# Key gathers of an AUGRU spread over its half steps, whole rows for the first steps, score rows on another queue, weights sorted after a branch

## The chip, the cores and the metric

The kernel runs on one core of one Trainium2 chip. The metric is device time of one execution in microseconds (us), lower is better. The engines named below are PE (matmul), DVE (vector), ACT (scalar, activations), POOL (GpSimd) and SP (mostly issues DMA transfers). A group of DMA transfers is issued on the queue of the engine that names it; gathers by a list of row numbers (indirect DMAs) are issued by POOL, one for 128 rows.

## The reference

1024 sequences of 100 items, 128 features each. Cut to what matters:

```python
# GRU over t: keys[:, t] = h after step t
def gru_step(h, x_t): ...                 # 3 gates, 128 -> 128, on x_t and h
keys = scan(gru_step, h0, items)
feat = concat([keys, q, keys - q, q * keys])      # q: the item embedding
score = mlp(feat, att_W0..W2, relu); score = where(mask, score, -inf)
attn = softmax(score, axis=time)
pooled = einsum('bt,btd->bd', attn, keys)
att_seq = pooled.T[:T]                    # feature t of a sequence weights step t
def augru_step(h, (x_t, a_t)):
    r = sigmoid([h, x_t] @ Wr.T + br); u = sigmoid([h, x_t] @ Wu.T + bu)
    h_hat = tanh([h * r, x_t] @ Wh.T + bh)
    u = a_t * u
    return (1 - u) * h + u * h_hat
aug = scan(augru_step, h0, keys with att_seq)
attention_feature = aug[at the sequence's length - 1]
out = mlp([user, item, hist_sum, item * hist_sum, attention_feature], ph_W0..W2, sigmoid)
```

## The kernel before, in words

Everything is kept transposed: features on 128 partitions, sequences along the free axis, in two halves of `HB` = 512 sequences that are worked in turn. One step of one half is called a half step.

**First phase, GRU** (to about 1580 us). The outer loop runs over t, the inner over the two halves. A half step has ten matmuls of 128x128 by 512 in f32 for the gates (L438) and a few for the attention score (L506, L507, L678). `transpose` turns the new state by 32x32 blocks on DVE into `kt` (L482), and every four steps one DMA on SP's queue stores the tile (128 partitions, 16 blocks of 32 sequences, 4 steps of 32 features each) to a table `keys_d` in DRAM (L485). `transpose` is followed two steps later by `score`, which spreads one row of `mv` into `s_b` by a DMA on SP's queue (L519); ACT's next write of `mv` (L510) waits for that DMA, and DVE's softmax in blocks reads `s_b`. On SP's queue stand also the loads of inputs `x` (L409) and masks `m` (L414). POOL accumulates `hist` and `pooled` (L425, L426, L598, L599).

**Between the phases.** `weights` forms `att` and stores it to `pooled_d` (L614), in pieces of 32 floats (128 B), on the queues of SP and ACT in turn. `features` and `sort_weights` follow: POOL gathers the rows of `pooled_d` in order of length (L114), PE turns them (L656), DVE copies the result (L658), SP stores it to `att_d`, a matmul with one row of the unit matrix spreads the weights of t = 0 (L661), and ACT copies them to `h3` (L668). Then each engine loads a number that says which of three lists of widths fits the lengths, and branches (L882, L883).

**Second phase, AUGRU** (`augru_phase`, from about 1622 us). Sequences are sorted by length, so a step works on the first w columns of a half only; w falls from 512 by about 5 a step from t = 3 on (482 at t = 8, 276 at t = 48, 30 at t = 96). A half step is six matmuls (L784 and L786: gates r, u and h, each on the key and on the state), three activations on ACT (L793, L796, L800) and five operations on DVE, of which L794 feeds the last matmul. The key of step t comes from the table in groups of steps, `READ` = 4, then 8 each, starting at `FIRST` = 0, 4, 12, 20 and so on. For each block of 32 columns of each half one gather brings 128 rows of 1 KB (32 features by 8 steps) into `rows` (L130). `load_group` issues all gathers of the next group one after the other when the loop reaches a group's first step; the 32 gathers of group 0 run early, during the GRU. `load_key`, two steps ahead, takes a step's key out of `rows` by 32x32 transposes on DVE (L772). `load_att` loads the weight row of a step (L762, SP's queue). When no sequence of a block of 128 is left, `predict` computes its outputs.

The work is written in this order in the program; a tile scheduler places waits and moves independent instructions, and buffer counts (`k3` 6, `u3` 3, `rows` 4) bound how far an engine runs ahead.

Of the kernel before, what the change touches and what calls it, by code (L numbers as in the profile page):

```python
# [19 lines left out]
P = 128  # L20
# [25 lines left out]

G = 4
READ = [G] + [2 * G] * ((T - G) // (2 * G))
FIRST = [sum(READ[:q]) for q in range(len(READ))]

# [12 lines left out]
def kernel(ctx: ExitStack, tc: tile.TileContext, a: dict, out: bass.AP):  # L63
# [18 lines left out]

    nc = tc.nc
# [3 lines left out]
    keys_d = [dram.tile([NK * P, n * R], F32, name=f"keys_d{q}") for q, n in enumerate(READ)]  # L87
# [35 lines left out]
    def load_rows(q, i, width, tiles):  # L123

        n = READ[q]
        r = rows[q, i] = tiles.tile(
            [P, KH, n * R], F32, tag="once" if q == 0 else "rows", name="rows"
        )
        for k in range(-(-width // R)):
            nc.gpsimd.indirect_dma_start(  # L130
# [11 lines left out]
    def gru_phase(pools):  # L142
# [62 lines left out]
        def load_later():  # L205
# [183 lines left out]
        class Half:  # L389
# [85 lines left out]
            def transpose(self, t):  # L475
# [36 lines left out]
            def score(self, t):  # L512
# [6 lines left out]
                nc.sync.dma_start(  # L519
# [83 lines left out]
            def weights(self):  # L603
# [9 lines left out]
                for p in range(P // R):  # L613
                    (nc.scalar if p % 2 else nc.sync).dma_start(  # L614
                        out=to[p], in_=att[p * R : (p + 1) * R]
                    )
# [31 lines left out]

        def sort_weights(i):


            r = xp.tile([P, GH, P], F32, tag="x", name="att_r")
            p = ps.tile([P, HB], F32, tag="g", name="pw")
            for g in range(GH):
                gather(r[:, g, :], pooled_d, g, i)
                nc.tensor.transpose(p[:, ts(g, P)], r[:, g, :], ident)  # L656
            att = hp.tile([P, HB], F32, tag="h", name="att_t")
            nc.vector.tensor_copy(att, p)  # L658
            nc.sync.dma_start(out=att_d[i], in_=att[:T, :])
            first = ps.tile([P, HB], F32, tag="g", name="first")  # L660
            nc.tensor.matmul(  # L661
                first,
                lhsT=ident[:, 0:1].to_broadcast([P, P]),
                rhs=att,
# [291 lines left out]
```

## Time and profile before

| | |
|---|---|
| median of 3 runs | 2459.59 us (2458.4 to 2460.04) |
| the profiled execution | 2471.84 us, its span 2470.0 us |
| mean PE clock granted in it | 0.932 |
| PE busy | 2211.2 us (90%) |
| DVE, POOL, ACT busy | 1723.1, 1276.1, 995.7 us |
| gathers of keys on POOL (L130) | 250, 961 ns each |

The profile comes from one execution. A row of the timeline gives the start and the length of an instruction in us, the engine, the line of the kernel (L130), the operation, what it writes and reads (`out<-in`), the shape and, in brackets, how long its engine had been idle and what it had been waiting for ("issue" is time in which it waited for nothing that the profile shows, "remote" a wait whose releaser is not known). Rows of the 40 slices give busy tenths of each fortieth of the span, about 62 us; PEclk is the clock that PE was granted, in tenths. A row of windows gives start and end, length, busy us and count of each engine, then PE's clock, the DMA engines' busy share and GB/s. A wait row gives the total in us, how often, and the longest.

### The profile page before, as it was taken

The page shows a single profiled execution, that of the slowest core. Times are in us where ns is not written, and L with a number is a line of the kernel's source. Part 1 is how long each engine was busy: PE and PEld are TensorE (multiplying, and loading weights), DVE is VectorE, ACT ScalarE, POOL GpSimd, SP SyncE. Part 2 cuts the span into 40 slices and gives each one's busy share as a digit, 9 for nine tenths or more (in the row PEclk, how much of TensorE's full clock was granted, in tenths as well). Part 3 has the DMA queues.
Part 4 walks back from the last instruction along what each step waited for, and adds up shares of the span by engine and source line. Part 5 has one row for each costly group of instructions (what it writes and reads, how often), then busy time and mean ns, then how long its engine had stood idle before and what let it go on. Part 6 is the DMA issues. An engine that isn't in the chain of part 4 may idle for free. (4 is left out here: it accounts for less than half of the span.)

```text
span 2470.0 us, 22200 instructions
## 1 busy us (share of the span) xinstructions
PE 2211.2 (90%) x6184; PEld 1093.0 (44%) x6184; DVE 1723.1 (70%) x3175; ACT 995.7 (40%) x1729; POOL 1276.1 (52%) x1121
## 2 busy tenths in 40 slices
PE   8998899999999999999999998544987898888898
PEld 3333333344444444444444443211433455667787
DVE  7798667777878777777777787722755666666652
ACT  3343344444444444444444444311332333344432
POOL 0169977666666666666666669364213303222200
PEclk9999999999999999999999999866988988999875
DMA  4533333322222323233222321232223212222210
GB/s 103 136 89 103 111 110 101 86 87 89 85 88 89 86 89 96 85 99 88 85 89 88 87 87 56 58 122 80 83 60 87 82 44 78 73 69 73 55 28 5
DMA packets 228009, 204.22 MB, mean 83 GB/s; under 512 B 41166, under 2 KB 190386, under 8 KB 227874
## 3 DMA queue, kind: packets, MB, share of 16 engines
q1 hardware_dynamic: 213122, 170.40, 24.3%
q0 software_dynamic: 12640, 32.04, 4.5%
q8 instruction: 50, 0.82, 0.1%
q14 instruction: 85, 0.70, 0.1%
q10 hardware_dynamic: 2112, 0.26, 0.1%
HBM read 146.60 MB, written 54.40 MB: 81 GB/s over the span
## 5 line engine op out<-in xcount | busy, mean ns | idle before, releaser
L438 PE MATMUL ps<-x,wih 128*128 128x512 f32 x1200 | 597.1, 607 | 20.2 <-ACT r L450 10.4
L438 PE MATMUL ps<-hn,whh 128*128 128x512 f32 x1188 | 576.0, 594 | 0.4 <-DVE hn L473 0.4
L130 POOL DMA_INDIRECT rows<-keys_d,idx_k x250 | 240.3, 961 | 480.6 <-DVE k L772 375.9
L438 PEld LDWEIGHTS ps<-x,wih 128*128 128x128 f32 x1200 | 221.1, 191 | 347.6 <-issue 272.1
L438 PEld LDWEIGHTS ps<-hn,whh 128*128 128x128 f32 x1188 | 226.0, 190 | 285.8 <-issue 275.6
L510 ACT ACTIVATE mv<-f 128x512 f32<-128x512 f32 x200 | 125.9, 630 | 468.9 <-DVE f L509 304.6
L425 POOL TENSOR_TENSOR xm<-x,m 128x512 f32<-128x512 f32 x200 | 249.6, 1264 | 75.7 <-DMA m<-mask_d 66.9
L786 PE MATMUL ph<-r,wh 128*128 128x512 f32 (+55 forms) x396 | 150.3, 465 | 148.5 <-DVE r L794 92.0
L469 ACT ACTIVATE ps<-ps,bih 128x512 f32<-128x512 f32 x200 | 132.2, 661 | 352.2 <-DVE ps L468 351.0
L599 POOL TENSOR_TENSOR pooled<-pooled,kw 128x512 f32<-128x512 f32 x190 | 258.4, 1360 | 6.7
L426 POOL TENSOR_TENSOR hist<-hist,xm 128x512 f32<-128x512 f32 x200 | 258.7, 1308 | 2.4
L458 DVE SCALAR_TENSOR_TENSOR u<-ps,bhh,r 128x512 f32<-128x512 f32 x198 | 145.6, 735 | 141.5 <-ACT r L450 137.8
L506 PE MATMUL pm<-hn,wk 128*128 128x512 f32 x400 | 209.4, 605 | 33.1 <-DVE f L509 14.8
L584 POOL TENSOR_TENSOR pooled<-pooled,e 128x512 f32<-128x512 f32 x25 | 28.9, 1156 | 385.0 <-ACT e L558 385.0
L471 DVE TENSOR_TENSOR d<-hn,ps 128x512 f32<-128x512 f32 x198 | 135.9, 686 | 119.3 <-ACT ps L469 116.3
L598 POOL TENSOR_TENSOR kw<-kt,e 128x512 f32<-128x512 f32 x190 | 210.9, 1128 | 0.5 <-DVE old L565 0.3
L507 PE MATMUL pm<-kq,wkq 128*128 128x512 f32 x400 | 207.0, 599 | 0.0
L504 DVE TENSOR_TENSOR kq<-hn,item 128x512 f32<-128x512 f32 x200 | 191.7, 958 | 1.3
L800 ACT ACTIVATE ph<-ph,bh 128x512 f32<-128x512 f32 (+48 forms) x200 | 91.9, 459 | 204.4 <-PE ph L786 137.4
L793 ACT ACTIVATE pr<-pr,br 128x512 f32<-128x512 f32 (+49 forms) x198 | 90.5, 457 | 181.9 <-PE pr L786 107.0
L786 PEld LDWEIGHTS ph<-r,wh 128*128 128x128 f32 x396 | 74.9, 217 | 194.9 <-DVE r L794 118.2
L796 ACT ACTIVATE pu<-pu,bu 128x512 f32<-128x512 f32 (+48 forms) x200 | 91.6, 458 | 154.6 <-PE pu L786 70.4
(143 smaller groups left out, 3396.7 us busy)
## 6 DMA issues: line engine op xcount, KB each, us to landing
x<-in_hist_x SPq DMA_DIRECT2D x212, 256.0 KB
keys_d<-kt SPq DMA_DIRECT2D x50, 1024.0 KB
m<-mask_d SPq DMA_DIRECT2D x200, 128.0 KB
rows<-keys_d,idx_k POOLq DMA_INDIRECT x250
s_b<-mv SPq DMA_DIRECT2D x200, 8.0 KB
mask_i<-in_mask SPq DMA_DIRECT2D x8, 200.0 KB
at<-att_d SPq DMA_DIRECT2D x4, 256.0 KB
part_d<-part SPq DMA_DIRECT2D x2, 400.0 KB
```

The lines of the kernel that those rows point to most:

```text
L130: nc.gpsimd.indirect_dma_start(out=r[:, k, :], out_offset=None, in_=keys_d[q], in_offset=bass.IndirectOffsetOnAxis(ap=idx_k[:, k, i : i + ...
L425: nc.gpsimd.tensor_mul(d, x, m)
L426: nc.gpsimd.tensor_add(acc, acc, d)
L438: nc.tensor.matmul(p, lhsT=w[:, g, :], rhs=v, start=(j == 0), stop=(j == len(parts) - 1),)
L458: nc.vector.scalar_tensor_tensor(out=u, in0=ph, scalar=bhh[:, 2:3], in1=r, op0=ALU.add, op1=ALU.mult,)
L471: nc.vector.tensor_sub(d, h, pi)
L504: nc.vector.tensor_mul(kq, h, item[:, self.cols])
L506: nc.tensor.matmul(p, lhsT=wk[i], rhs=h, start=True, stop=False)
L507: nc.tensor.matmul(p, lhsT=wkq[i], rhs=kq, start=False, stop=True)
L598: eng.tensor_mul(d, k, w)
L599: eng.tensor_add(acc, acc, d)
L786: nc.tensor.matmul(p, lhsT=m[:, 0, :], rhs=v, start=False, stop=True)
```

## The change

Five parts.

1. `READ` starts 4, 4, 8, ... For groups 0 and 1 (t = 0 to 7, `WHOLE` = 2) the table holds whole rows of 128 features by 4 steps. `transpose` stores them by four DMAs of 32x16x32 in each half step of t = 0 to 7 (64 in all, 512 pieces of 128 B each) where one of the old form stood for each four steps. One gather brings 128 whole rows of 2 KB, four for a half, and `load_key` turns the key on PE (four transposes) and copies it on ACT.
2. The gathers of the later groups are drawn from a generator, `RATE` = 2 in each half step, and what is left of a group when its predecessor's first step comes is issued at once. Ahead of each gather, from step 1 on, POOL copies one column of the latest `u` into the gather's target, so that the gather waits for that half step's DVE instruction. `load_key` runs one step ahead instead of two. In the AUGRU there are 204 gathers of the old form (250 before, 32 of them early), 8 of whole rows there and 8 early.
3. The `s_b` rows are issued on ACT's queue.
4. `sort_weights` moves behind the branch, after the keys and the gate matmuls of t = 0 (`first_step`); the stores to `pooled_d` are all on SP's queue.
5. `rank`'s comparison and sum become one DVE instruction each.

```diff
-READ = [G] + [2 * G] * ((T - G) // (2 * G))
+WHOLE = 2
+READ = [G] * WHOLE + [2 * G] * ((T - WHOLE * G) // (2 * G))
+READ += [T - sum(READ)] * (sum(READ) < T)
 FIRST = [sum(READ[:q]) for q in range(len(READ))]
+RATE = 2
...
-    keys_d = [dram.tile([NK * P, n * R], F32, name=f"keys_d{q}") for q, n in enumerate(READ)]
+    keys_d = [
+        dram.tile([B, n * P] if q < WHOLE else [NK * P, n * R], F32, name=f"keys_d{q}")
+        for q, n in enumerate(READ)
+    ]
...
     def load_rows(q, i, width, tiles):
 
         n = READ[q]
-        r = rows[q, i] = tiles.tile(
-            [P, KH, n * R], F32, tag="once" if q == 0 else "rows", name="rows"
-        )
+        if q < WHOLE:
+            tag = "whole" if q else "once"
+            r = rows[q, i] = tiles.tile([P, GH, n * P], F32, tag=tag, name="rows")
+            for g in range(GH):
+                gather(r[:, g, :], keys_d[q], g, i)
+                yield
+            return
+        r = rows[q, i] = tiles.tile([P, KH, n * R], F32, tag="rows", name="rows")
         for k in range(-(-width // R)):
+            if later.get("pace") is not None:
+
+                nc.gpsimd.tensor_copy(r[:, k, 0:1], later["pace"])
             nc.gpsimd.indirect_dma_start(
...
                 nc.vector.tensor_scalar(
-                    above, order, own[:, g : g + 1], None, ALU.is_gt
-                )
-                nc.vector.tensor_reduce(rank[:, g : g + 1], above, AX.X, ALU.add)
+                    above,
+                    order,
+                    own[:, g : g + 1],
+                    0.0,
+                    ALU.is_gt,
+                    ALU.add,
+                    accum_out=rank[:, g : g + 1],
+                )
...
-                if n == G - 1:
-                    row, part = divmod(q + 1, 2) if q else (0, 0)
+                if q < WHOLE:
+                    to = keys_d[q][self.cols, :].rearrange(
+                        "(k r) (n a c) -> n a r k c", r=R, n=G, c=R
+                    )
+                    for p in range(P // R):
+                        nc.sync.dma_start(
+                            out=to[n, p], in_=kt[p * R : (p + 1) * R, :, n, :]
+                        )
+                elif n == G - 1:
+                    row, part = divmod(q - WHOLE, 2)
                     nc.sync.dma_start(
-                        out=keys_d[row].rearrange("(k p) m -> p k m", p=P)[
+                        out=keys_d[WHOLE + row].rearrange("(k p) m -> p k m", p=P)[
                             :, self.ks, ts(part, G * R)
                         ],
                         in_=kt.rearrange("p k n c -> p k (n c)"),
...
-                nc.sync.dma_start(
+                nc.scalar.dma_start(
                     out=s_b.rearrange("(p r) f -> p r f", r=R)[:, s - b0, :],
...
-                    (nc.scalar if p % 2 else nc.sync).dma_start(
-                        out=to[p], in_=att[p * R : (p + 1) * R]
-                    )
+                    nc.sync.dma_start(out=to[p], in_=att[p * R : (p + 1) * R])
...
-        for i in range(NH):
-            sort_weights(i)
-
     def augru_phase(pools, widths):
...
-        keys, att = {}, {(0, i): h3[i] for i in range(NH)}
+        keys, att = {}, {}
+        later["pace"] = None
+
+        def first_step(i):
+
+            k = keys.pop((0, i))
+            gates = []
+            for n, f in (("u", AF.Sigmoid), ("h", AF.Tanh)):
+                p = ps.tile([P, HB], F32, tag="g", name=f"p{n}")
+                nc.tensor.matmul(p, lhsT=later["w" + n][:, 1, :], rhs=k, start=True, stop=True)
+                nc.scalar.activation(p, p, f, bias=later["b" + n])
+                gates.append(p)
+            return gates
+
+        def sort_weights(i):
+            r = wp.tile([P, GH, P], F32, name="att_r", bufs=2)
...
         def load_key(t, i):
 
             q = max(j for j, first in enumerate(FIRST) if first <= t)
-            w = -(-widths[t] // R)
-            k = wp.tile([P, KH, R], F32, name="k3", bufs=6)
-            nc.vector.transpose(
-                k[:, :w, :], rows[q, i][:, :w, ts(t - FIRST[q], R)]
-            )
-            k = k.rearrange("p k r -> p (k r)")
+            w, n, r = widths[t], t - FIRST[q], rows[q, i]
+            k = wp.tile([P, HB], F32, name="k3", bufs=6)
+            if q < WHOLE:
+                p = ps.tile([P, HB], F32, tag="g", name="pk3")
+                for g in range(-(-w // P)):
+                    nc.tensor.transpose(p[:, ts(g, P)], r[:, g, ts(n, P)], ident)
+                nc.scalar.copy(k[:, :w], p[:, :w])
+            else:
+                w = -(-w // R)
+                nc.vector.transpose(
+                    k.rearrange("p (k r) -> p k r", r=R)[:, :w, :], r[:, :w, ts(n, R)]
+                )
             keys[t, i] = k
...
             nc.vector.tensor_mul(u, pu, at)
+            later["pace"] = u[:, 0:1]
...
-        def load_group(q):
+        def gathers(q):
             for i in range(NH):
-                all_of(load_rows(q, i, widths[FIRST[q]], kp))
-
-        load_group(1)
-        for t in range(2):
-            for i in range(NH):
-                load_key(t, i)
+                yield from load_rows(q, i, widths[FIRST[q]], kp)
+
         for i in range(NH):
+            load_key(0, i)
+        gates = [first_step(i) for i in range(NH)]
+        for i in range(NH):
+            sort_weights(i)
+        all_of(gathers(1))
+        ahead = gathers(2)
+        for i in range(NH):
+            load_key(1, i)
             load_att(1, i)
         for t in range(T):
-            if t in FIRST[1:-1]:
-                load_group(FIRST.index(t) + 1)
+            if t in FIRST[2:-1]:
+                all_of(ahead)
+                ahead = gathers(FIRST.index(t) + 1)
             for i in range(NH):
                 if t + 2 < T:
                     load_att(t + 2, i)
-                step(t, i)
-                if t + 2 < T:
-                    load_key(t + 2, i)
+                if t:
+                    step(t, i)
+                else:
+                    pu, ph = gates[i]
+                    u = wp.tile([P, HB], F32, name="u3")
+                    nc.vector.tensor_mul(u, pu, h3[i])
+                    nc.vector.tensor_mul(h3[i], u, ph)
+                for _ in range(RATE):
+                    next(ahead, None)
+                if 1 < t + 1 < T:
+                    load_key(t + 1, i)
```

How the instructions stand on POOL around the branch and the start of the AUGRU, before (`att_r` are the weights' gathers, `part` belongs to `predict`, `keys_d_61` and so on are the tables of groups 1 and later, x25 means 25 in a row):

```order
L114 DMA att_r<-pooled_d,idx 128x128 x8
L882 TENSOR_LOAD over_d
L883 COMPARE_AND_BRANCH
...
L130 DMA rows<-keys_d_61,idx_k 128x256 x25
L130 DMA rows<-keys_d_62,idx_k 128x256 x30
L114 DMA part_11613<-part_d,idx 128x200
L114 DMA part_11634<-part_d,idx 128x200
L130 DMA rows<-keys_d_63,idx_k 128x256 x28
L130 DMA rows<-keys_d_64,idx_k 128x256 x24
```

And now:

```order
L934 COMPARE_AND_BRANCH
...
L123 DMA att_r<-pooled_d,idx 128x128
L123 DMA rows<-keys_d_61,idx 128x512 x8
L147 DMA rows<-keys_d_62,idx_k 128x256 x4
L123 DMA part_11805<-part_d,idx 128x200
L123 DMA part_11826<-part_d,idx 128x200
L146 COPY rows<-u_10367 128x1 x2
L147 DMA rows<-keys_d_62,idx_k 128x256 x2
L146 COPY rows<-u_10399 128x1 x2
L147 DMA rows<-keys_d_62,idx_k 128x256 x2
```

The weights' gathers moved behind the branch, 8 whole-row gathers and 4 key gathers follow them, and from there on two gathers stand behind two copies of one half step's `u`.

On PE at the same place, before (`pu`, `ph`, `pr` are the gates' sums, `k` a key, `h` a state):

```order
L656 MATMUL pw<-ident,att_r 128x128 x4
L661 MATMUL first<-att_t,ident 128x512
L656 MATMUL pw<-ident,att_r 128x128 x4
L661 MATMUL first<-att_t,ident 128x512
L882 TENSOR_LOAD over_d
L883 COMPARE_AND_BRANCH
L784 MATMUL pu<-k_10291,wu 128x512
L784 MATMUL ph<-k_10291,wh 128x512
```

And now (`pk` is a key being turned):

```order
L934 COMPARE_AND_BRANCH
L812 MATMUL pk_10255<-ident,rows 128x128 x4
L812 MATMUL pk_10262<-ident,rows 128x128 x4
L770 MATMUL pu<-k_10254,wu 128x512
L770 MATMUL ph<-k_10254,wh 128x512
L770 MATMUL pu<-k_10261,wu 128x512
L770 MATMUL ph<-k_10261,wh 128x512
L782 MATMUL pw<-ident,att_r 128x128 x4
L787 MATMUL first<-att_t,ident 128x512
L782 MATMUL pw<-ident,att_r 128x128 x4
L787 MATMUL first<-att_t,ident 128x512
L812 MATMUL pk_10323<-ident,rows 128x128 x4
```

The key and gate matmuls of t = 0 moved ahead of the weights' transposes, and the keys of t = 1 are turned on PE after them.

More of the change, by code (lines that the diff above doesn't have):

```diff
@@ L647, in features @@
                 )
[L649 to L664, printed above, removed]
-                start=True,
-                stop=True,
-            )
-            nc.scalar.copy(h3[i], first)
         halves = [Half(i) for i in range(NH)]
@@ L756, in augru_phase @@
         wr, wu, wh = later["wr"], later["wu"], later["wh"]
-        keys, att = {}, {(0, i): h3[i] for i in range(NH)}
+        keys, att = {}, {}
[11 more added lines that the diff above has]
+            r = wp.tile([P, GH, P], F32, name="att_r", bufs=2)
+            p = ps.tile([P, HB], F32, tag="g", name="pw")
+            for g in range(GH):
+                gather(r[:, g, :], pooled_d, g, i)
+                nc.tensor.transpose(p[:, ts(g, P)], r[:, g, :], ident)
+            rows_t = wp.tile([P, HB], F32, name="att_t", bufs=2)
+            nc.vector.tensor_copy(rows_t, p)
+            nc.sync.dma_start(out=att_d[i], in_=rows_t[:T, :])
+            first = ps.tile([P, HB], F32, tag="g", name="first")
+            nc.tensor.matmul(
+                first,
+                lhsT=ident[:, 0:1].to_broadcast([P, P]),
+                rhs=rows_t,
+                start=True,
+                stop=True,
+            )
+            nc.scalar.copy(h3[i], first)
         def load_att(t, i):
```

26 lines of the change are left out of this document (10 added, 16 removed).

## The prediction

> **What bounds the kernel now.** I read the page first: the busy lines and the slices tell which engine carries which stage.
>
> ```profile
> PE 2211.2 (90%) x6184; PEld 1093.0 (44%) x6184; DVE 1723.1 (70%) x3175; ACT 995.7 (40%) x1729; POOL 1276.1 (52%) x1121
> ...
> PE   8998899999999999999999998544987898888898
> ...
> PEclk9999999999999999999999999866988988999875
> ...
> L130 POOL DMA_INDIRECT rows<-keys_d,idx_k x250 | 240.3, 961 | 480.6 <-DVE k L772 375.9
> ```
>
> TensorE (PE) carries the GRU (slices 1 to 25). From slice 26 on PE is no longer full and its clock (PEclk) falls now and then: those are the places to look at. Next I read busy time by stretches; the first is GRU, the second to fourth lie in the AUGRU.
>
> ```profile
> 600.00:1500.00 900.00, 893.98 (x2151) 367.07 (x2150) 707.09 (x1115) 421.29 (x645) 606.20 (x494) 1.00 0.30 88
> ...
> 1628.00:1723.00 95.00, 41.24 (x76) 16.97 (x75) 24.87 (x38) 12.71 (x20) 57.10 (x60) 0.69 0.35 107
> 1723.00:1768.00 45.00, 45.00 (x110) 20.64 (x109) 34.97 (x55) 17.79 (x28) 0.03 (x1) 1.00 0.17 50
> ```
>
> The columns after the length are busy time and count on PE, weight loads, DVE, ACT and POOL, then PE clock, DMA share and GB/s. In the AUGRU PE is full while POOL is quiet (1723 to 1768) and works less than half of the time while POOL gathers (1628 to 1723). The gathers come in bursts, all of a group back to back. The timeline of the second AUGRU burst, POOL first, then ACT, then PE, shows what a burst does:
>
> ```profile
> 1767.97 0.95 POOL L130 DMA_INDIRECT rows<-keys_d,idx_k  x1 [64.89 <-DVE k L772]
> ...
> 1802.25 0.95 POOL L130 DMA_INDIRECT rows<-keys_d,idx_k  x1 [0.30 <-issue]
> ```
>
> ```profile
> 1769.02 0.64 ACT L793 ACTIVATE pr<-pr,br 128x482 f32<-128x482 f32 x1 [0.98 <-PE pr L786]
> ...
> 1780.23 0.63 ACT L796 ACTIVATE pu<-pu,bu 128x476 f32<-128x476 f32 x1 [0.96 <-issue]
> 1785.12 0.63 ACT L800 ACTIVATE ph<-ph,bh 128x476 f32<-128x476 f32 x1 [4.25 <-PE pu L786]
> 1790.78 0.63 ACT L793 ACTIVATE pr<-pr,br 128x472 f32<-128x472 f32 x1 [5.04 <-remote]
> 1798.47 0.63 ACT L796 ACTIVATE pu<-pu,bu 128x472 f32<-128x472 f32 x1 [7.06 <-issue]
> ```
>
> ```profile
> 1784.80 0.95 PE L784 MATMUL ph<-k,wh 128*128 128x472 f32 x2
> 1792.14 1.94 PE L786 MATMUL ph<-r,wh 128*128 128x472 f32 x2 [6.39 <-issue]
> ```
>
> The 28 gathers run from 1767.97 to 1802.25, 1.27 us from start to start (0.95 busy, 0.30 between). ACT does three activations per half step. The first eight after the burst's start come on time, 1.6 us apart (1769.02 to 1780.23); the ninth is 3.3 us late, and the next come 5.7 and 7.7 us apart, although the matmul that they read is long done. PE stands idle, then resumes at half pace (1.94 against 0.95 for the same pair). The first burst shows the same count:
>
> ```profile
> 1622.71 0.95 POOL L130 DMA_INDIRECT rows<-keys_d,idx_k  x1 [6.05 <-ACT h L668]
> ```
>
> ```profile
> 1635.67 0.66 ACT L793 ACTIVATE pr<-pr,br 128x512 f32<-128x512 f32 x1 [1.05 <-issue]
> 1639.71 0.66 ACT L796 ACTIVATE pu<-pu,bu 128x512 f32<-128x512 f32 x1 [3.38 <-PE ph L784]
> ```
>
> The activation at 1635.67 is the eighth after 1622.71, and the ninth is the first late one. Eight free activations and then a trickle look as if ACT's supply of instructions is held while POOL works off gathers, and ACT lives on what it has queued: 8/3 = 2.7 half steps.
>
> The Trainium skill ("Advanced Engine Details and Errata", section "Engine Queue Depths") gives ScalarE a queue of 8 instructions; the trace's eight on-time activations agree.
>
> **What the bursts cost.** In the start of the AUGRU, step 1 begins at 1628.60 and, six half steps on, step 4 at 1722.51.
>
> ```profile
> 1628.60 1.02 PE L784 MATMUL pr<-k,wr 128*128 128x512 f32 x2
> ...
> 1633.75 1.02 PE L784 MATMUL pr<-k,wr 128*128 128x512 f32 x2
> ```
>
> ```profile
> 1722.51 1.00 PE L784 MATMUL pr<-k,wr 128*128 128x502 f32 x2
> ```
>
> ```profile
> 1664.66 0.71 DVE L772 STREAM_TRANSPOSE k<-rows 128x512 f32<-128x512 f32 x1 [13.29 <-DMA rows<-keys_d,idx_k]
> ```
>
> An undisturbed half step is 1633.75 − 1628.60 = 5.15 us, six are 30.9; the stretch took 93.9: 63 us lost to 62 gathers and two part rows, about 1.0 us a gather. Part of it is DVE's wait for the first gathers (13.29 us). For the ten later bursts I compare ten stretches with a burst in them and the ten between (PE alone; first, last and sum of ten each).
>
> ```profile
> 1768.00:1820.00 52.00, 35.25 (x77) 0.84 0.35 101
> ...
> 2355.00:2370.00 15.00, 12.36 (x85) 0.89 0.27 59
> sum 308.00, PE 212.02; mean PE 21.20
> ```
>
> ```profile
> 1723.00:1768.00 45.00, 45.00 (x110) 1.00 0.17 50
> ...
> 2330.00:2355.00 25.00, 21.84 (x162) 1.00 0.18 34
> sum 339.00, PE 334.18; mean PE 33.42
> ```
>
> The burst stretches hold 724 matmuls in 308 us, the quiet ones 1306 in 339, or 0.260 us each. At that rate the 724 need 188 us: 120 us lost, for 156 gathers (28, 24, 22, 20, 16, 14, 12, 10, 6, 4), 0.77 each. Checked on the first: 77 matmuls at 45/110 us need 31.5 of its 52.
>
> **The change, part by part.** The terms are for the profiled execution, 2471.84 us with a span of 2470.0; it lies 12.25 above the median of 2459.59, and I take the sum off the median.
>
> *Start of the AUGRU: −63, and +9 that stays.* Group 1 is now 8 gathers of whole rows for t 4 to 7 in place of 32 that step 2 waited for, and the 30 of the next group are spread. What remains in a row behind the branch, by the order shown above, is 8 of the weights, 8 whole rows, 4 key gathers and 2 part rows: 22 × 1.26 = 28 us, from 1606.85 to about 1634. If the eight-deep supply holds, ACT spends it on the first step's gates and copies, and step 1 starts near 1634 rather than at the 1625 worked out below: +9. Bounds: 0 (none of them matters), and the 14 that follow the weights at the start's 1.0 us, 14.
>
> *Later bursts: −90 of 120.* Each half step now issues two gathers behind a copy that waits for that step's `u`: POOL holds ACT some 2.5 us, then nothing until the next `u`. At the 5.15 us half step three activations must be supplied in the other 2.6 us; one per 5.7 to 7.7 us is the held rate, the free one must be at least ACT's own, so for wide steps I take no stall. Twelve matmul records make a half step: 45/110 × 12 = 4.9 us in the first quiet stretch, 25/162 × 12 = 1.9 in the last. From about t = 48 (width 276, 5.15 × 276/512 = 2.8) it is below the 2.5 to 2.8 of a pair; POOL then gathers without a break for a group's first half steps, and the 56 gathers of those groups (16, 14, 10, 8, 6 and 2 by the widths) cost up to today's 0.77 each, 43; a stalled step delays its own next pair, which halves it to 22, and some 8 go to cold restarts of PE: 30. Bounds: 0, and everything that is there now (120). The copy of 128x1 itself is not in the trace; on POOL it lies between the 0.30 between gathers and a gather's 0.95, twice in a half step, and POOL waits anyway. `u` has three buffers, so DVE would wait for POOL only when POOL is three half steps behind.
>
> *Transposes of whole rows on PE: +14.* Keys of t = 1 to 7 need 7 × 2 × 4 = 56 transposes on PE in place of DVE's. Ends: a 512-column pass at steady pace is 5.15/12 = 0.43 us, a quarter of it 0.107; alone and cold one took 0.47 (below). So 6 to 26; they stand between warm passes, nearer the lower end: 0.25, 14 us. ACT gets a copy each, some 0.6 us, in a half step in which ACT is 40% busy: covered, unless supply is short.
>
> *Weights behind the branch: −3.*
>
> ```profile
> 1598.22 5.55 ACTq L614 DMA_DIRECT2D pooled_d<-att  x4
> ...
> 1606.85 1.00 POOL L114 DMA_INDIRECT att_r<-pooled_d,idx  x1 [21.00 <-DMA pooled_d<-att]
> ...
> 1609.38 0.47 PE L656 MATMUL pw<-ident,att_r 128*128 128x128 f32 x1 [27.03 <-DMA att_r<-pooled_d,idx]
> ...
> 1621.60 0.59 ACT L668 COPY h<-first 128x512 f32<-128x512 f32 x1 [4.37 <-PE first L661]
> 1622.68 1.28 ACT L796 ACT_TABLE_LOAD   x1 [0.50 <-issue]
> ```
>
> Now the weights run from 1606.85 to 1622.2 (1621.60 + 0.59), and after them table load and first step until 1628.60: 6.4 us. Behind the change the branch, table load and gates of t = 0 lie in the wait for `pooled_d` (21 us idle on POOL), and only two products on DVE for each half follow, about 2.8 us: 1625, 3.6 less, of which the stores on one queue take back some: −3. Ends 0 and −6.4.
>
> *GRU: −15.*
>
> ```profile
> 1598.00:1603.00 5.00, 0.00 (x0) 0.00 (x0) 4.80 (x11) 0.00 (x0) 0.00 (x0) 0.50 0.35 52
> 1603.00:1607.00 4.00, 0.00 (x0) 0.00 (x0) 0.00 (x0) 0.00 (x0) 0.15 (x1) 0.50 0.44 66
> 110.00:340.00 230.00, 205.37 (x473) 82.04 (x472) 179.65 (x260) 93.06 (x142) 171.94 (x147) 0.96 0.34 99
> ```
>
> ```profile
> ACT mv L510 <- DMA s_b<-mv: 150.8, 22, 13.7
> ```
>
> ```profile
> 320.83 3.78 PE L438 MATMUL ps<-x,wih 128*128 128x512 f32 x4 [4.96 <-ACT r L450]
> ```
>
> ```profile
> q1 hardware_dynamic: 213122, 170.40, 24.3%
> ```
>
> The score rows (`s_b`) wait behind other loads on SP's queue; ACT waits for them 22 times, up to 13.7 us, and PE stands 4.96 us behind one such wait. PE idles 24.6 us between 110 and 340 and 6.0 between 600 and 1500. On ACT's queue the rows issue at once: of these 30.6 I take half, −15. Against it: 200 issues on ACT (at most 5.55/4 = 1.39 us each, ACT 47% busy between 600 and 1500, so covered), and 64 stores in pieces of 128 B for t < 8 where 4 with larger pieces stood: 32768 pieces. The `pooled_d` stores have the same pattern: 4096 pieces in 5.0 × 0.35 + 4.0 × 0.44 = 3.5 us of 16 engines, 14 ns a piece; the queue's mean is 0.243 × 16 × 2470 us/213122 = 45 ns. That is 28 to 92 us of all engines over some 120 us that are 34% used: share 0.57, or at the far end over 1, with loads of `x` then some 13 us late. Ends −30 and +20. Taking the accumulate into one DVE instruction in `rank` lies beside PE's matmuls: 0.
>
> The Trainium skill ("DMA: Bandwidth & Descriptors", section "Specifications") says that pieces under 512 B fall off line rate by a read-modify-write; by it the far end would hold, and this term would be near −2 in place of −15. The `pooled_d` stretch above, 14 ns a piece, does not show it.
>
> *Second group's last gathers: +2.* They are paced by step 7 and read at step 8, hardly a half step later; a gather's data come 2.5 us after its start (`att_r` above: 1606.85, read at 1609.38), once.
>
> Sum: −63 + 9 − 90 + 14 − 3 − 15 + 2 = −146: 2471.8 − 146 = 2325.8 for a profiled execution like that one, **2314 us** for the median.
>
> **The rivals.**
> - *No stall is left.* Eight queued activations bridge every pair, narrow steps too: the 30 and the 9 go, the transposes cost 8: −191, 2269 us. For it speaks that the first eight activations of each burst lost nothing at all; against, the width of late steps.
> - *The price is per gather, spread or not.* The mean of both parts is 183/218 = 0.84, the later bursts' 0.77. The 204 key gathers, 8 whole rows and 2 parts would cost 0.77 × 214 = 165 where 183 went: −18 + 14 − 3 − 15 + 2 = −20, 2440 us. For it: the price per gather is alike in long and short bursts; against: each burst's first ten gathers cost nothing.
> - *Slower: each pair starves ACT and PE restarts cold.* If a pair at every half step leaves no time for refilling, the price is that of the start, 1.02 us a gather: 218 − 183 − 2 = +33, 2493 us. It decides from 185/214 = 0.86 us a gather on. Against: 1723 to 1768 shows that ACT needs only 40% of the time.
> - *In GRU the small stores bind*: the +20 end in place of −15: 2349 us.
>
> **How the numbers follow.** Forecast 0.42, no stall left 0.25, small stores 0.08, price per gather or part of it 0.19, slower 0.06. The forecast's own range is 2280 to 2350 by the ends of transposes and GRU. 8 in 10 reach from under the no-stall case (its transposes at 6 and GRU at −30 give 2252) to halfway into the price per gather: 2248 to 2400. A measurement of this kernel tells about 0.2% (5 us) from no change: faster 0.91, same 0.03 (a price per gather of 0.84 to 0.88), slower 0.06.
>
> **What would show it.** POOL's gathers in pairs with a copy ahead, one pair a half step; PE full from 1640 to about 2050 with steps of 5.15 us and PEclk near 1.0; ACT waits on "remote" gone but for the start and the narrow steps; `s_b` no longer in ACT's waits; transposes under 0.3 us. The prediction is wrong if ACT still waits 2 us or more in each wide half step, if PE's pauses follow the pace of POOL, or if loads of `x` come late in the first 8 steps.

## The result, and the profile after

| | before | after |
|---|---|---|
| median | 2459.44 us (4 runs, 2458.4 to 2460.04) | 2330.97 us (4 runs, 2330.42 to 2333.93) |
| profiled execution | 2471.84 us, span 2470.0 | 2330.42 us, span 2328.6 |
| mean PE clock | 0.932 | 0.959 |

The ratio is 0.9481, 95% interval [0.9464, 0.9497]: 128.5 us faster, on a chip where the kernel before takes some 2460 us. That such a chip must be named is a finding of the experiments; on two other chips the kernel before takes 2300 us and the change brings 0.3%.

The page after, its lines of PE and of PE's clock in 40 slices of 58 us each:

```profile
PE   8997789999999999999999999995899999998888
...
PEclk9999899999999999999999999997899999999975
```

The notches that followed each burst in the AUGRU (slices 30 on) are gone; the one that is left, at slices 28 and 29, is the seam between the phases and the start. The dip early in the GRU, slices 4 and 5, is deeper than before. Windows of the profile after: the first two half steps, the next ten with paced pairs, then wide steps, then narrow ones before width 128 (length, busy us and count of PE, weight loads, DVE, ACT, POOL, then PE's clock).

```profile
1637.00:1658.00 21.00, 15.39 (x34) 7.07 (x34) 5.12 (x9) 4.88 (x8) 12.37 (x17) 0.83 0.64 202
1658.00:1713.00 55.00, 55.00 (x161) 26.62 (x160) 33.78 (x51) 24.20 (x40) 21.00 (x39) 1.00 0.30 90
1728.00:1795.00 67.00, 66.12 (x170) 32.39 (x171) 52.92 (x87) 26.15 (x42) 31.22 (x56) 1.00 0.36 104
2144.00:2206.00 62.00, 52.29 (x315) 46.68 (x314) 41.23 (x150) 26.84 (x80) 21.06 (x36) 0.92 0.28 72
```

From 1658 to 1713 POOL gathers in every half step (21 of 55 us busy) and PE is full at full clock; in the kernel before PE was busy for 41 of 95 us while POOL gathered. The rows of POOL's timeline there show what the pacing is: a pair of copies when `u` is there, two gathers, then a wait.

```profile
1674.41 0.31 POOL L146 COPY rows<-u 128x1 f32<-128x1 f32 x2 [2.64 <-DVE u L838]
1675.10 0.97 POOL L147 DMA_INDIRECT rows<-keys_d,idx_k  x1 [0.39 <-POOL rows L146]
1676.38 0.95 POOL L147 DMA_INDIRECT rows<-keys_d,idx_k  x1 [0.31 <-issue]
1679.96 0.31 POOL L146 COPY rows<-u 128x1 f32<-128x1 f32 x2 [2.62 <-DVE u L838]
```

Below, the time that a half step takes over 5.15 us × w/512 is taken from the starts of its first matmul (`pr` on the key), for widths over 130; it is called its loss. The spans then differ by these terms:

| stretch | before | after | difference |
|---|---|---|---|
| GRU, to the end of the wait for `pooled_d` (before: POOL's, after: ACT's) | 1606.85 | 1619.84 | +13.0 |
| from there to step 1 | 21.75 | 17.04 | −4.7 |
| loss of steps 1 to 7 | 63.1 | 15.3 | −47.8 |
| loss from step 8 to width 130, outputs' work included | 155.0 | 56.4 | −98.6 |
| the rest, below width 130 | 125.6 | 122.2 | −3.3 |

Together −141.4, the difference of the spans. From step 1 on 150 us are won, the stretch ahead of it gives 5, and the GRU takes 13 back.

### The profile page after: what moved, and what is told of

Its sections match the earlier page's. It is cut to its first block, busy times and chain, and to the rows that moved or that the text cites. A ratio compares the mean times of both kernels' runs of the same rounds, so it can differ in the third digit from the quotient of the medians.

```text
span 2328.6 us, 22713 instructions
## 1 busy us (share of the span) xinstructions
PE 2191.2 (94%) x6248; PEld 1087.1 (47%) x6248; DVE 1706.5 (73%) x3159; ACT 1005.1 (43%) x1743; POOL 1273.1 (55%) x1291
## 5 line engine op out<-in xcount | busy, mean ns | idle before, releaser
L460 PE MATMUL ps<-x,wih 128*128 128x512 f32 x1200 | 601.8, 611 | 36.9 <-ACT r L472 19.7
L447 POOL TENSOR_TENSOR xm<-x,m 128x512 f32<-128x512 f32 x200 | 234.3, 1187 | 103.0 <-DMA m<-mask_d 96.2
L448 POOL TENSOR_TENSOR hist<-hist,xm 128x512 f32<-128x512 f32 x200 | 269.0, 1360 | 2.8
L147 POOL DMA_INDIRECT rows<-keys_d,idx_k x204 | 196.2, 962 | 70.7 <-issue 39.8
L694 ACT ACTIVATE mv<-px,bx 41x512 f32<-41x512 f32 x202 | 137.2, 679 | 158.5 <-DMA m<-mask_d 91.1
L146 POOL COPY rows<-u 128x1 f32<-128x1 f32 x200 | 30.7, 181 | 285.1 <-DVE u L838 281.2
L828 PE MATMUL ph<-r,wh 128*128 128x512 f32 (+55 forms) x396 | 140.5, 439 | 26.6 <-DVE r L834 15.9
L472 ACT ACTIVATE r<-ps,brz 128x512 f32<-128x512 f32 x200 | 136.3, 682 | 49.7 <-PE ps L460 30.6
L841 ACT ACTIVATE ph<-ph,bh 128x512 f32<-128x512 f32 (+49 forms) x198 | 90.5, 457 | 153.2 <-PE ph L828 138.1
```

Source lines behind the costliest of these rows:

```text
L147: nc.gpsimd.indirect_dma_start(out=r[:, k, :], out_offset=None, in_=keys_d[q], in_offset=bass.IndirectOffsetOnAxis(ap=idx_k[:, k, i : i + ...
L447: nc.gpsimd.tensor_mul(d, x, m)
L448: nc.gpsimd.tensor_add(acc, acc, d)
L460: nc.tensor.matmul(p, lhsT=w[:, g, :], rhs=v, start=(j == 0), stop=(j == len(parts) - 1),)
L694: nc.scalar.activation(half.mv[r, :], p[r, :], AF.Relu, bias=bx[r, :])
L828: nc.tensor.matmul(p, lhsT=m[:, 0, :], rhs=v, start=False, stop=True)
```

## The experiments

**Pacing taken away, pacing alone, a faster pace, score rows put back.** These four ran on one chip, where the kernel before took 2464.83 us.

*Without the copies of `u`:*

```diff
             nc.vector.tensor_mul(u, pu, at)
-            later["pace"] = u[:, 0:1]
```

> The changed kernel without the copies of u ahead of the gathers: still two gathers per half step in program order, but POOL no longer waits for the step, so a group's gathers run back to back as soon as their buffers are free. Theory 1 (a long row of gathers on POOL holds back ACT's instructions, its queue of 8 bridges 2.7 half steps; only spacing cures it): the stalls of the later bursts come back, 132 us of them in place of the 36 that the changed kernel has, and the 32 gathers of group 2 follow the start in one row, some 15 to 25 more: about 2425 to 2455 us. Rival (the gain comes from the whole rows at the start and from fewer gathers, pacing does little): 2330 us, within 10.

Measured 2477.61 us, ratio 1.006 [1.0037, 1.0083]: without the copies all is lost, and a little more. The losses of steps 1 to 7 are 83.8 and from step 8 on 137.9 us. On ACT's timeline, in the row of gathers that follows the start:

```profile
1671.54 0.59 ACT L813 COPY k<-pk 128x512 f32<-128x512 f32 x1 [10.56 <-remote]
1682.80 0.66 ACT L833 ACTIVATE pr<-pr,br 128x512 f32<-128x512 f32 x1 [10.68 <-remote]
1693.97 0.66 ACT L836 ACTIVATE pu<-pu,bu 128x512 f32<-128x512 f32 x1 [10.51 <-remote]
```

One instruction of ACT each 11 us; in the first burst of the kernel before it was one each 10 to 11 us (1668.41, 1678.91, 1689.41). The time is 22 us over the range expected: later steps lose 81.5 us more than in the changed kernel, less than the 96 expected, but the row of group 2 behind the start, counted at 15 to 25 us, costs 68.5.

*The kernel before with pacing alone:*

```diff
         for k in range(-(-width // R)):
+            if later.get("pace") is not None:
+                nc.gpsimd.tensor_copy(r[:, k, 0:1], later["pace"])
             nc.gpsimd.indirect_dma_start(
...
-                load_group(FIRST.index(t) + 1)
+                all_of(ahead)
+                ahead = gathers(FIRST.index(t) + 1)
...
+                for _ in range(RATE):
+                    if t >= FIRST[1]:
+                        next(ahead, None)
-                if t + 2 < T:
-                    load_key(t + 2, i)
+                if 1 < t + 1 < T:
+                    load_key(t + 1, i)
```

> The kernel before with only the pacing added: two gathers a half step behind a copy of u from step 4 on, keys one step ahead instead of two; stores, whole rows, score rows, weights as before. Theory 1: the later bursts' stalls fall from 132 to about 36 us, and the start keeps only its first 32 gathers and two parts instead of 62 (63 falls to some 35): 2459 - 96 - 28 = 2335 us, plus up to 2 us for each of 11 groups whose last gathers come late: 2335 to 2357. Rival (whole rows at the start are what counts): 2400 or more.

Measured 2331.81 us, ratio 0.9454 [0.9438, 0.947]. Pacing alone gives all that the change gives (ratio 0.9481, on another chip of the same kind); its other four parts cancel. Against the changed kernel step 1 starts 7.9 us earlier (1628.97), steps 1 to 7 lose 26.2 us, 10.9 more, and later ones 51.4, 5.0 less; the GRU ends where it did before (its last score activation starts at 1570.87, before at 1570.66).

*Four gathers in a half step:*

```diff
-RATE = 2
+RATE = 4
```

> The changed kernel with four gathers per half step instead of two, each still behind a copy of u. Theory 1: four in a row hold ACT for 5.0 of the 5.15 us of a wide half step, so the queue of 8 is not refilled and runs out after 2 to 3 half steps; a group of 32 then stalls for most of its length, limited by the wait for u: between a quarter and all of the 96 us come back, 2355 to 2425 us. Rival (a gather costs what it costs, or nothing, whatever its neighbours): 2331 us, within 5.

Measured 2405.02 us, ratio 0.975 [0.9733, 0.9766]. Four pairs of copy and gather are longer than a half step, so POOL gathers without a break again (the first 20 from 1740.67 to 1767.17), and 64 of the later steps' 99 us come back (loss from step 8 on 120.8). Spacing, and not the wait for `u` as such, is what counts.

*Score rows on SP's queue again:*

```diff
-                nc.scalar.dma_start(
+                nc.sync.dma_start(
                     out=s_b.rearrange("(p r) f -> p r f", r=R)[:, s - b0, :],
```

> The changed kernel with the score rows s_b issued on SP's queue again. The changed kernel's GRU was 35 us behind at step 20 and 15 behind at its end. Theory A (ACT's queue gives back 20 us from step 20 on, the early loss is from SP's queue and the whole-row stores): the 20 us are lost again, about 2350 us. Rival B (score rows on ACT's queue block ACT early, 7.9 us at 201 to 209 us, and are what costs): the GRU is earlier, 2315 to 2325 us.

Measured 2322.1 us, ratio 0.9425 [0.941, 0.9441], against 0.9481 for the change on its chip. The GRU ends as in the kernel before (last score activation at 1570.31, against 1585.99 in the changed kernel), with the 64 stores in 128-byte pieces in it, so these and the shorter `rank` together cost nothing; neither was run alone. Step 1 starts at 1623.13, 5.5 us earlier than before. So rival B holds. Where the score rows on ACT's queue do harm is seen in the changed kernel at 201 us, and again from 310 us on:

```profile
201.41 7.89 ACTq L549 DMA_DIRECT2D s_b<-mv  x2
209.35 0.69 ACT L472 ACTIVATE r<-ps,brz 128x512 f32<-128x512 f32 x1 [10.61 <-DMA place_i<-inv_d]
```

```profile
309.90 0.62 ACT L540 ACTIVATE mv<-f 128x512 f32<-128x512 f32 x1
321.28 0.50 ACTq L549 DMA_DIRECT2D s_b<-mv  x1
321.83 0.68 ACT L694 ACTIVATE mv<-px,bx 41x512 f32<-41x512 f32 x1 [11.31 <-DMA m<-mask_d]
```

Two issues hold ACT's queue for 7.89 us, and at 321.28 an issue goes out only after ACT has stood for 11.31 us; each time the GRU's next activations stand behind them. From 110 to 400 PE idles 46.6 us in the changed kernel, 26.8 in this run and 27.6 in the kernel before. A wait of DVE for an index load on SP's queue (`place_i`), 15.0 us in the changed kernel, is no part of the difference: this run has it too (18.6 us; 3.8 in the kernel before). What the issues waited for was not tested; nor were score rows on ACT's queue without the small stores.

**Packets, plain loads, a busy POOL.** The next four ran on a chip where the kernel before took 2301.33 us, 163 us less than on the one above. So they cannot tell the theories apart; they show the other kind of chip.

*Eight gathers in every fourth half step, sixteen in every eighth:*

```diff
-                for _ in range(RATE):
+                for _ in range(8 if (2 * t + i) % 4 == 2 else 0):
```

```diff
-                for _ in range(RATE):
+                for _ in range(16 if (2 * t + i) % 8 == 6 else 0):
```

> The changed kernel with its gathers in packets: eight behind one u in every fourth half step, instead of two in each. The mean rate is the same, the row is 8 x 1.26 = 10 us long, two wide half steps, in which ACT needs 6 to 8 instructions. Theory 1 (ACT lives on a queue of 8 while gathers run): the queue just covers it, so no or little time is lost in wide steps: 2325 to 2345 us. Rival (what counts is how much of a half step POOL is busy with gathers, or any row longer than two stalls): the price of four in a row or more, 2380 to 2405 us.

> As the run before, with sixteen gathers in every eighth half step: the row is 20 us, four wide half steps, in which ACT needs 12 instructions and has 8. Theory 1: each row of 16 stalls once the queue is empty, after some 13 us, for the rest of the row and a trickle: some 8 to 12 us for each of about 14 such rows in the wide steps and less later, 2410 to 2450 us. Rival (only the mean rate counts): 2331 us.

Measured 2319.91 (ratio 1.0075 [1.0051, 1.01]) and 2405.01 us (1.0451 [1.0434, 1.0469]). The second number looks like the stall that was expected and is another: the 16 gathers stand right ahead of the step that reads them. With eights DVE also waits for late rows, 21.9 us between 1710 and 2200 (5.7 in the changed kernel on such a chip, shown further below). The waits with sixteens, 1720 to 1900 us:

```profile
DVE k L816 <- DMA rows<-keys_d,idx_k: 32.8, 4, 14.1
```

```profile
1764.48 0.62 ACT L836 ACTIVATE pu<-pu,bu 128x466 f32<-128x466 f32 x1 [0.94 <-PE pu L828]
...
1783.00 0.61 ACT L836 ACTIVATE pu<-pu,bu 128x456 f32<-128x456 f32 x1 [0.92 <-PE pu L828]
```

DVE waits up to 14.1 us for rows that are late; ACT, on its timeline, starts 13 activations between these two rows, both included, one each 1.5 to 1.6 us, while a row of sixteen gathers runs (from 1763.26 on). So on this chip a row of sixteen gathers does not hold ACT.

*Plain loads in place of gathers, and POOL filling a scratch tile beside them:*

```diff
-RATE = 2
+RATE = 64
...
-            nc.gpsimd.indirect_dma_start(
...
+            nc.gpsimd.memset(scr, 0.0)          # second kernel only
+            nc.sync.dma_start(out=r[:, k, :], in_=keys_d[q][ts(i * KH + k, P), :])
```

> The changed kernel without pacing and without gathers for the groups from t = 8 on: the same blocks of 128 rows of 1 KB are loaded in unsorted order by ordinary DMAs on SP's queue, a whole group as soon as the step before it starts (so the outputs are those of other rows). The bytes, the pieces and the bursts are those of the run without pacing. Theory 1 (it is POOL's work on a gather that holds ACT): no stalls at all, transposes and predictions alone: 2285 to 2320 us. Rival (the traffic of a burst or its landing in SBUF stalls the engines): as without pacing, 2440 to 2480 us.

> As the run before, and POOL also works: for each block left to SP it fills a scratch tile of 128x1024 once, 0.94 us each as in the profile before, a group's fills in one row behind the first u of the group (so the outputs are those of other rows). Theory 1a (only the making of descriptors holds ACT): as the run before, within 10 us. Theory 1b (any long row of work on POOL holds the other engines): the stalls of the run without pacing, 2430 us or more.

Measured 2286.29 (0.9937 [0.992, 0.9953]) and 2289.88 us (0.9942 [0.9924, 0.9961]). Neither stalls, but on this chip rows of gathers don't either: inconclusive.

**All forms in one kernel, and the change on the second kind of chip.** Before took 2300.44 us here, on yet another chip.

```diff
+MODE = {3: "burst", 4: "plain", 5: "fill", 6: "eight", 7: "burst", 8: "plain", 9: "fill"}
```

> One kernel with every way of loading a group in one profile, since the runs before were on two chips: on one the kernel before takes 2465 us, on the other 2301. From the changed kernel: group 2 (t = 8 on) in paced pairs, group 3 as one row of 28 gathers, group 4 by plain DMAs on SP's queue, group 5 by plain DMAs and a row of 24 fills of 0.94 us on POOL, group 6 in packets of eight, group 7 as one row of 18 gathers, group 8 plain, group 9 plain and fills, the rest paced pairs (groups 4, 5, 8 and 9 get rows in unsorted order). Where the kernel before is slow (near 2460): theory 1a (only rows of gathers hold the engines): groups 3 and 7 lose some 20 and 13 us, the plain ones, the fills and the packets under 2 each; theory 1b (any row of work on POOL): the fills lose as much as the gathers; traffic theory: the plain ones lose too. Where the kernel before is fast (near 2300): no group loses more than 2, the rows of gathers neither, since the hold is not there on that chip.

> The changed kernel itself, to be compared with the kernel before on this chip. Where the kernel before is near 2460 us: 2330, ratio 0.948. Where it is near 2300 us (no hold): pacing then has nothing to win, the late GRU (+13) and the transposes (+5) remain against the earlier start (-5): 2305 to 2325 us, ratio 1.00 to 1.01.

The mixed kernel took 2297.26 us in its one execution, the changed kernel 2293.89, ratio 0.9968 [0.9957, 0.998]. The gain on such a chip is 6.6 us; the time is 11 us under the range expected. No trace of the kernel before was taken on such a chip, so what the change still wins there stays open. The window of the mixed kernel with the last 19 of its row of 28 gathers, PE never idle:

```profile
1726.00:1771.00 45.00, 45.00 (x116) 21.85 (x115) 36.17 (x60) 17.95 (x29) 17.87 (x19) 1.00 0.55 157
```

And the changed kernel here, the stretches that answer to the first and last window shown above:

```profile
1638.00:1659.00 21.00, 21.00 (x59) 10.09 (x59) 11.39 (x17) 9.09 (x15) 15.41 (x22) 0.99 0.75 244
...
2116.00:2178.00 62.00, 58.21 (x376) 52.90 (x374) 49.83 (x179) 32.56 (x95) 22.45 (x39) 1.00 0.33 79
```

59 matmul records in the first 21 us against 34, and 376 against 315 in the last 62 us before width 128: what the changed kernel still loses on the first kind of chip is the same hold, at the start (losses of steps 1 to 7: 5.6 against 15.3) and in narrow steps (36.9 against 56.4 from step 8 on; the difference lies from t = 48 on, 20.3 against 43.1).

*Score rows on SP's queue for 24 steps, on ACT's after; one gather a half step in narrow groups:*

```diff
+LATE = 24
-                nc.scalar.dma_start(
+                (nc.scalar if s >= LATE else nc.sync).dma_start(
...
-                for _ in range(RATE):
+                for _ in range(RATE if widths[min(t + 8, T - 1)] > 7 * R else 1):
```

> The changed kernel with score rows on SP's queue for the first 24 steps and on ACT's after, and one gather per half step instead of two for groups that fit (14 gathers or fewer). Theory: the early loss of 35 us in the GRU goes, the 15 us won at the GRU's end stay, so it ends 30 us earlier than the changed kernel's, and narrow steps lose some 10 us less: 2330 - 30 - 10 = 2290 us, 2280 to 2305. Rival (the 15 us at the end only make up for the early loss and are not there without it): 2310 to 2320 us, like the run with all score rows on SP's queue.

Measured 2268.5 us beside 2293.89 for the changed kernel on the same chip, ratio to before 0.9862 [0.984, 0.9885]: better than both. Step 1 starts at 1602.88 against 1637.96, the last score activation at 1552.25. The last score activation is 18 us earlier than with all rows on SP's queue (1570.31) and 35 earlier than with all on ACT's (1587.54 on this chip): ACT's queue is worth 18 us late in the GRU and costs 35 early. That cost is good to some 7 us, since the mixed kernel, whose GRU is the same, ends its GRU at 1580.38 on this chip. The expected time had been worked out for the first kind of chip. The single gathers lose 6 us on this one (42.6 against 36.9 from step 8 on), where 10 were to be won; this kernel was not run on the first kind.

*The mixed kernel again, with the score rows split like that:*

> The mixed kernel again, with score rows on SP's queue for the first 24 steps and on ACT's after. Where the kernel before is near 2460 us (the hold is there): theory 1a: the rows of 28 and of 18 gathers lose some 20 and 13 us, the start some 10, the groups loaded by plain DMAs, the fills on POOL and the packets of eight under 2 each, time 2290 to 2310 us; theory 1b: the fills lose some 18 and 10 as well; traffic: the plain groups too. Where the kernel before is near 2300 us: no row of gathers loses anything, and the earlier GRU alone shows: 2297 - 34 = 2263 us, 2258 to 2270; against 2268.5 for the kernel with single gathers in narrow steps, this tells whether the singles cost some 5 us there.

This ran where the kernel before took 2465.7 us: 2341.1 us, ratio 0.9495 [0.9469, 0.9521]. Windows in this order: the row of 28 gathers, plain loads (two windows), fills, the row of 18 gathers, fills in narrow steps.

```profile
1703.00:1748.00 45.00, 24.01 (x50) 10.73 (x49) 16.82 (x28) 7.51 (x12) 23.70 (x25) 0.72 0.34 97
1748.00:1790.00 42.00, 42.00 (x110) 20.68 (x109) 33.35 (x56) 16.73 (x27) 0.00 (x0) 1.00 0.46 131
1790.00:1858.00 68.00, 68.00 (x190) 35.85 (x189) 55.02 (x96) 28.01 (x48) 0.00 (x0) 1.00 0.34 97
1858.00:1886.00 28.00, 28.00 (x85) 15.90 (x84) 22.83 (x43) 11.80 (x21) 17.53 (x21) 1.00 0.18 50
2007.00:2036.00 29.00, 15.70 (x52) 10.65 (x51) 11.36 (x26) 6.30 (x13) 12.32 (x13) 0.76 0.32 90
2108.00:2140.00 32.00, 32.00 (x166) 29.44 (x165) 28.98 (x83) 17.37 (x41) 13.70 (x16) 1.00 0.20 48
```

Only the two rows of gathers leave PE idle: 24.01 busy of 45, 15.70 of 29. The plain loads move more (131 GB/s against 97) and cost nothing; POOL is as busy with fills as with gathers and costs nothing. In losses: the row of 28 some 24 us (0 in the same kernel on the other chip), the row of 18 some 16 (0), the packets of eight 8.3 (5.2 there, from data that come late), so 3 for 20 gathers. ACT in the row of 28:

```profile
1712.40 0.63 ACT L844 ACTIVATE pr<-pr,br 128x476 f32<-128x476 f32 x1 [1.12 <-PE pr L839]
1721.52 0.63 ACT L847 ACTIVATE pu<-pu,bu 128x476 f32<-128x476 f32 x1 [8.48 <-remote]
1732.02 0.63 ACT L852 ACTIVATE ph<-ph,bh 128x476 f32<-128x476 f32 x1 [9.87 <-remote]
```

DVE is late as well, with a transpose that waited for nothing the profile shows; PE did its ready matmuls on time until 1719 and then stood behind DVE:

```profile
1727.12 0.68 DVE L827 STREAM_TRANSPOSE k<-rows 128x480 f32<-128x480 f32 x1 [4.23 <-issue]
```

```profile
1740.38 1.95 PE L839 MATMUL ph<-r,wh 128*128 128x476 f32 x2 [20.99 <-DVE r L845]
```

Theory 1a is shown, for ACT and DVE: on this kind of chip a long row of indirect DMAs on POOL holds them, not the bytes moved and not POOL's being busy. One difference was not varied: the plain loads read their rows in order, the gathers scattered; paced pairs read scattered rows too and cost nothing in wide steps. The time of the whole, 2341, is over the 2290 to 2310 expected. Against the profiled execution of the first mixed kernel (2297.26, this one 2343.28) step 1 starts 24.5 us earlier and not 34, steps 1 to 7 lose 9.3 more, the later ones 57.6 more (the two rows 40 in place of 33, the packets 3, and narrow steps, which the guess had left out), and the rest takes 3.6 more: 46.0.

## Why the prediction was right, and where it was off

The forecast was 2314 us, 2248 to 2400; the time was 2331. By its own steps:

- *Start, −63 + 9 = −54.* Measured −47.8 for the losses, with the transposes in it (5.3); without them −53. The 9 us were put down to a late step 1; step 1 was not held, but the first two half steps took 10.26 and 10.68 us in place of 5.15, 10.6 together, while 22 gathers stood in a row. The same two half steps lose 0.7 and 0.4 us on the other kind of chip, so it is the hold: cause and size right, place one step off.
- *Later bursts, −90 of 120.* Measured −98.6, and −3.3 below width 130. The mechanism held: from step 8 on, stalls stay only from t = 48 on, where a half step (2.8 us at width 276) is shorter than a pair with its copies (2.9 us, 1674.41 to 1677.33 above). A comparison with the same kernel on the other kind of chip shows it: 43.1 us are lost against 20.3 from t = 48 on, and 13.3 against 16.6 in steps 8 to 47. So some 23 us of hold stay, where 30 were forecast.
- *Transposes, +14.* Four take 0.44 us in each half step, 0.11 each: PE's rows of the changed kernel, step start to step start 5.55 where 5.11 is the width's share.

```profile
1674.41 0.60 PE L812 MATMUL pk<-ident,rows 128*128 128x128 f32 x4
1674.85 1.02 PE L827 MATMUL pr<-k,wr 128*128 128x508 f32 x2
...
1680.40 1.01 PE L827 MATMUL pr<-k,wr 128*128 128x502 f32 x2
```

  It is the lower end (0.107), 5 us for steps 1 to 7. The term was mis-sized, 14 for 5: between warm passes there was no reason to go to twice the share.
- *Weights behind the branch, −3.* Measured −4.7, but not for the reason given. The gates of t = 0 did not run in the wait for `pooled_d`: ACT's copy of the first key waited for that very transfer.

```profile
1619.84 1.07 ACT L813 COPY k<-pk 128x512 f32<-128x512 f32 x2 [13.04 <-DMA pooled_d<-att]
```

  They ran beside the weights' gathers instead. The key's tile is new and probably lies where the last phase's `att` was; that was not tested.
- *GRU, −15.* This step failed: it took +13.0. "On ACT's queue the rows issue at once" did not hold early on, where two issues held ACT 7.89 us; the cover named for them (ACT 47% busy) is none, since an issue that waits held all behind it. The run with the rows on SP's queue shows it: with it the GRU is where it was, and the split one has both the 18 us and no early loss. The small stores, a rival by themselves, cost nothing there, together with the shorter `rank`: the read-modify-write that the Trainium skill ("DMA: Bandwidth & Descriptors", "Specifications") states for pieces under 512 B shows no cost in time here.
- *Second group's last gathers, +2.* Measured 2.1, in the two half steps of t = 8.
- *From the profiled execution to the median.* The sum was −146 against −141.4 measured on the profiled executions, 4.6 apart. The other 12.7 us come from taking it off the median of before, which was 12.25 below its profiled execution; after, the two agree within 0.6.
- *Luck.* That the sum came within 4.6 us is in part luck: the GRU was 28 us worse than forecast, and start with transposes (8), later bursts (14) and weights (2) were together some 23 better. The chip was luck too: the sum had no term for it, and on the other kind of chip the same change brings 6.6 us.
- *The forecast's own range.* "2280 to 2350 by the ends of transposes and GRU" is added wrongly: by those ends it is 2291 to 2361.

Of the rivals, "no stall is left" holds on the second kind of chip only; "the price is per gather" and "each pair starves ACT" are excluded for wide steps by the window from 1658 to 1713, where pairs cost nothing. The reading of the eight on-time activations as a queue (the Trainium skill, "Advanced Engine Details and Errata", "Engine Queue Depths") fits the packets of eight, which cost some 3 us for 20 gathers where a row of 28 cost 24. It also fits that what passes on time is a number and not a stretch of time: in the seven bursts of the kernel before from 1767.97 to 2228.07 it is 8, 7, 7, 7, 6, 6 and 6 activations, while the last of them starts 12.3 us into the burst in the first and 4.5 in the last. It is not always eight, then (five in the mixed kernel's row of 28), and "each burst's first ten gathers cost nothing" does not hold in narrow steps. That ACT lacks instructions, rather than signals, in a hold was argued and not shown: the profile only calls the releaser remote.

## What to carry to other kernels

A long row of indirect DMAs on POOL can stop engines that do not wait for its data; here two in each step, tied to the step by a tiny copy, cost nothing as long as the step is longer than the pair (2.9 us with its copies). Look for it where ACT's gaps end "remote" while POOL gathers. A transfer put on a computing engine's queue can block that engine while its issue waits, here for 7.89 and 11.31 us: choose the queue by phase and not by kernel. And a gain of this kind must be measured on more than one chip: here it is 5.2% on some and 0.3% on another.

## What was not expected of the hardware

The kernel before took 2459 to 2466 us in the first comparison and on two of the experiments' chips, and 2300 to 2301 on two others, the timed runs on each within 0.3% of their median. The same mixed kernel, but for its score rows, lost 24 us to a row of 28 gathers on one chip and nothing on another, at the same 1.25 us from gather to gather. What sets the kind (the chip, or where the program lies in it) stays open.
